# Spacing the four loads of a weight part, and a later limit for the angle tables, in an attention and convolution kernel

## The chip, the cores and the metric

The kernel runs on one core of a Trainium2 chip. The metric is the device time of one execution in microseconds (us). Before the change it is 2664.18 us, the median of three runs (2663.63 to 2665.53).

## What is computed

Four images of 1024 channels and 32 x 32 positions, so 1024 tokens each, go through an attention layer and then a bottleneck of convolutions. All numbers are float32. Shortened:

```python
# layer 0: attention, 16 heads of 64
q, k, v = split(x @ w_qkv.T + b_qkv)
q, k = rmsnorm(rope(q)) * q_norm_w, rmsnorm(rope(k)) * k_norm_w   # rope: rotation by angles
ctx = softmax(q @ k.T * 64 ** -0.5) @ v
x = x + rmsnorm(ctx @ w_proj.T) * norm_out_w
# layer 1: 1x1 (1024 -> 256), 3x3 (256 -> 256), 1x1 (256 -> 1024)
h = relu(bn(conv1(x))); h = relu(bn(conv2(h)))
return relu(x + softplus(residual_scale) * bn(conv3(h)))
```

## The kernel before

**Stages.** Everything runs in one loop over the four images: project q, then k, then v, then attention, then the output projection; the convolutions follow after the last image. The engines work in the order in which the Python program emits their instructions: the order of TensorE, VectorE, ScalarE and GpSimd (Pool) is written out by hand. Each of these takes its own list strictly in turn, so a step that waits holds up all that stands behind it on its engine. SP's queue issues most of the loads; Pool's queue issues the others, and nearly all stores of prepared weights.

**Projections.** Each projection is a product of 1024 x 1024 matrices, made with seven products of 2 x 2 blocks instead of eight (Strassen's way, in Winograd's form). This needs sums of weight blocks. `project` (q and k of the first image) uses one level. There, `operands` (L229) loads four blocks of weights by SP, makes four sums on VectorE (L236 to L239) and stores the results to `wd` in DRAM by Pool (L242). `project2` (all others) uses two levels: seven outer products, `OUTER`, each of seven inner ones, with sums of sums that are kept in `wd2`. The inner weights come by SP: three blocks by `quarter` (L383), from the weights themselves or from `wd`, and four from `wd2` (L472).

**Weight parts.** The sums for `wd2`, and the sums of the v weights for `wd`, are prepared while the first image is projected, and for one part while the second is. Each such part is made by `prepare` (L385, sums L392 to L395, stores L397) or `prepare_blocks` (L401, sums L409 to L412, stores L414). It takes four pieces of 256 KB in a buffer that is free at that time (`rq`, `unused`, `t`, `to`), issues four loads on Pool's queue one after the other, and returns a function `make`, which does four sums on VectorE and four stores on Pool. `unused` lies in the buffer of the first image's k, so the first write to k waits until the stores of `unused` have landed. `prepare_there` (L422 and following) makes sums of what lies in `rq` already.

**Pace.** `product_done` (L257) is called after each product of TensorE and counts the pace: 1 unit a product of four matmuls of 512 columns in `project`, 0.5 units a product in `project2`. `after(n, step)` puts a step on a list; the next call of `product_done` at which the pace has reached the due time emits it. Steps that are due together go in the order of their due times. A step of which the due time is now is not emitted at once, but by the next call. `weight_parts` (L1140) starts part i at `first + i * step` and lets its `make` follow `lag` = 4 units later. The calls that matter:

- first image, q: the four parts of the v weights for `wd`, then the v parts 0, 1 and 6, from pace 8 on, 2.4 apart (L1196); during k, q part 0 (L1209); during v, q parts 6 and 2, 6.5 units apart (L1216)
- second image, q: k part 5 (L1198)

Of the parts that are prepared during attention, by `load_parts`, the loads go by SP's queue.

**Semaphores.** Every DMA of Pool's queue takes one of eight completion semaphores in turn. It waits until the DMA that had the semaphore before, mostly the one eight places ahead in Pool's list, has landed.

**Angle tables.** `rope` (L709) multiplies q or k with tables of sines and cosines, `sinT` and `cosT`. The tables are first multiplied by the inverse norm of each token (L715), so they are spoilt and loaded anew by Pool after the last turn (L729). `pace["tables"]` (L730) is the pace before which the next rope may not start: the pace at the reload plus 3.7.

Of the kernel before, what the change touches and what calls it, by code (L numbers as in the profile page):

```python
# [18 lines left out]
P = 128  # L19
# [15 lines left out]
WQ, WK, WV, WP, W1 = 0, NFB, 2 * NFB, 3 * NFB, 4 * NFB  # L35
# [26 lines left out]
NH = NT // 2  # L62
NG = NT // 2
# [22 lines left out]
def program(ctx, tc, x, wblk, w2, w3, vecs, cos, sin, out, bad):  # L86


    nc = tc.nc
# [26 lines left out]
    def col(name, i=0):  # L116
        return vec[:, COL[name] + i : COL[name] + i + 1]
# [40 lines left out]
    with tc.tile_pool(name=f"st{u}", bufs=2) as st, ExitStack() as s:  # L158
# [14 lines left out]
        def load_tables(queue):  # L173
            for i in range(2):

                queue.dma_start(sinT[i::2, :], sin[1 - i :: 2, :])
            queue.dma_start(cosT, cos)
# [32 lines left out]
        def big_temp(name):  # L210
            return big.tile([P, N], F32, tag="big", name=name)

        def load_x(b, c, rows=range(NT)):
            for i in rows:
                nc.sync.dma_start(xs[b][:, i, half[c]], x[b, i * P : (i + 1) * P, half[c]])
# [33 lines left out]
        pace = {"at": 0, "room": 0.0, "hold": False, "tables": 0.0}  # L249
# [4 lines left out]
        def after(n, step):  # L254
            later.append((pace["at"] + n, step))
# [118 lines left out]
        def quarter(t, base, k, oq, iq, queue=nc.sync):  # L374

            ob, ih = {"A11": (0, 0), "A12": (0, 1), "A22": (1, 1)}.get(OUTER[k], (None, None))
            if ob is None:
                at = base // NT * NG + 2 * oq
                src = wd[at : at + 2, SUMS.index(OUTER[k]), :, iq * QT : (iq + 1) * QT]
            else:  # L380
                at = base + ob * NG + 2 * oq
                src = wblk[at : at + 2][:, :, ih * CH + iq * QT : ih * CH + (iq + 1) * QT]
            queue.dma_start(t.rearrange("p (g f) -> p g f", g=2), src.rearrange("g p f -> p g f"))  # L383

        def prepare(which, base, k, alloc, queue):  # L385

            a11, a12, a21, a22 = a = alloc(f"pre_{which}_{k}")
            for i, t in enumerate(a):
                quarter(t, base, k, i // 2, i % 2, queue)

            def make():
                nc.vector.tensor_tensor(a22, a21, a22, ALU.add)  # L392
                nc.vector.tensor_tensor(a21, a11, a21, ALU.subtract)
                nc.vector.tensor_tensor(a11, a22, a11, ALU.subtract)
                nc.vector.tensor_tensor(a12, a12, a11, ALU.subtract)  # L395
                for m, t in enumerate((a11, a22, a21, a12)):
                    nc.gpsimd.dma_start(wd2[which, k, m], t)  # L397

            return make

        def prepare_blocks(base, g, alloc, queue):  # L401

            a11, a12, a21, a22 = a = alloc(f"blk_{base}_{g}")
            for i, t in enumerate(a):
                ih = i % 2
                queue.dma_start(t, wblk[base + g + NG * (i // 2)][:, ih * NH * P : (ih + 1) * NH * P])

            def make():
                nc.vector.tensor_tensor(a22, a21, a22, ALU.add)  # L409
                nc.vector.tensor_tensor(a21, a11, a21, ALU.subtract)  # L410
                nc.vector.tensor_tensor(a11, a22, a11, ALU.subtract)
                nc.vector.tensor_tensor(a12, a12, a11, ALU.subtract)  # L412
                for o, t in enumerate((a11, a22, a21, a12)):
                    nc.gpsimd.dma_start(wd[base // NT * NG + g, o], t)  # L414

            return make

        def stay(tile, g):

            return lambda name: [tile[:, 2 * o + g // 2, half[g % 2]] for o in (0, 3, 2, 1)]  # L420
# [263 lines left out]
        def inverse_rms(total, eps, scale, name, then):  # L684


            r = temp(f"rms_{name}")[:, :QT]
            row = inv_d[norms_done.pop(0)]

            def root():  # L690
                o = bank("o2" if name in ("q_0", "k_0") else "o1", f"ss_{name}")[:, :QT]
                for q in range(4):
                    nc.tensor.matmul(
                        o[q * QH : (q + 1) * QH, :], ones[:, :QH], total[:, q * QT : (q + 1) * QT],
                        start=True, stop=True,
                    )
                nc.scalar.activation(r, o, AF.Sqrt, bias=eps, scale=scale)
                after(0.5, invert)

            def invert():  # L700
                spend(3 * TT)
                nc.vector.reciprocal(r, r)
                nc.gpsimd.dma_start(row.rearrange("(q t) -> q t", q=4), r[::QH, :])
                nc.gpsimd.dma_start(total, row.partition_broadcast(P))
                after(2.5, then)

            after(4, root)

        def rope(b, dst, total, eps, scale, w, tag, biased=True):  # L709

            def tables():
                for t in (sinT, cosT):
                    nc.vector.tensor_tensor(t, t, total, ALU.mult)  # L715

            def turn(f):
                k, other = dst[:, f, :], big_temp(f"{tag}s_{b}_{f}")
                for i, (t, table) in enumerate(((other, sinT), (k, cosT))):
                    if w is not None:  # L720
                        nc.vector.scalar_tensor_tensor(t, k, w[i][:, f : f + 1], table, ALU.mult, ALU.mult)
                    elif biased:
                        nc.vector.tensor_tensor(t, k, table, ALU.mult)
                    else:
                        nc.vector.scalar_tensor_tensor(t, k, col("bq", f), table, ALU.add, ALU.mult)
                for i in range(2):
                    nc.gpsimd.dma_start(dst[i::2, f, :], other[1 - i :: 2, :], accum_op=ALU.add)
                if f == NT - 1 and (b, tag) != (B - 1, "k"):
                    load_tables(nc.gpsimd)  # L729
                    pace["tables"] = pace["at"] + 3.7  # L730

            def then():
                if pace["at"] < pace["tables"]:
                    after(pace["tables"] - pace["at"], then)
                    return
                waiting.append((4 * TT, tables))
                for f in range(NT):
                    waiting.append((4 * TT, lambda f=f: turn(f)))

            inverse_rms(total, eps, scale, f"{tag}_{b}", then)  # L740
# [391 lines left out]
        def v_room(name):  # L1132
            return kv.tile([P, N // P, C], F32, tag="v", name=name)
# [6 lines left out]
        def weight_parts(parts, first, step, lag, alloc):  # L1140

            for i, part in enumerate(parts):
                after(first + i * step, lambda part=part: after(lag, part(alloc, nc.gpsimd)))

        def pieces_of(tile, cols=NCH):

            at = deque(tile[:, i, h] for i in range(tile.shape[1]) for h in half[:cols])

            def alloc(name):
                at.rotate(-4)  # L1150
                return [at[i] for i in range(-4, 0)]

            return alloc


        parts_of = {
            base: [
                lambda alloc, queue, which=which, base=base, k=k: prepare(which, base, k, alloc, queue)
                for k in range(len(OUTER))
            ]  # L1160
            for which, base in enumerate((WQ, WV, WP, WK))
        }

        def blocks_of(base):
            return [lambda alloc, queue, g=g: prepare_blocks(base, g, alloc, queue) for g in range(NG)]

        vector_and_act = {mybir.EngineType.DVE, mybir.EngineType.Activation}
        regions = ExitStack()
# [12 lines left out]
        room = v_room("rq_0")  # L1181
        for b in range(B):
# [8 lines left out]
            if b == 0:  # L1191
                unused = kp.tile([P, NT, N], F32, tag="k", name="unused")
                parts = [
                    lambda alloc, queue, g=g: prepare_blocks(WV, g, stay(room, g), queue) for g in range(NG)
                ]
                weight_parts(parts + [parts_of[WV][k] for k in (0, 1, 6)], 8, 2.4, 4, pieces_of(unused))  # L1196
            elif b == 1:
                weight_parts([parts_of[WK][5]], 9, 0, 4, pieces_of(room[:, : NT // 2, :]))  # L1198
# [24 lines left out]
            if b == 0:  # L1223
                todo = blocks_of(WP) + [parts_of[WP][k] for k in (0, 1, 6, 2, 3, 4, 5)]
                todo += [parts_of[WQ][k] for k in (1, 3, 4, 5)] + [parts_of[WK][k] for k in (0, 1, 6, 2, 3, 4)]
# [30 lines left out]
            room = v_room(f"to_{b}")  # L1256
# [12 lines left out]
            if b + 1 < B:  # L1269
# [3 lines left out]
                for j in range(NT):  # L1273

                    def load(b=b, i=rows[j]):
                        for c in range(NCH):
                            load_x(b + 1, c, (i,))
# [397 lines left out]
```

## Time and profile before

| view | value |
|---|---|
| median of 3 runs | 2664.18 us |
| profiled execution | 2667.97 us |
| its span, first to last instruction | 2666.2 us |
| mean granted clock of TensorE | 0.997 |
| VectorE waiting for sinT, in 3 places | 14.4 us |
| TensorE idle in the first 30 us (first x) | 5.9 us |
| DMA to landing, loads of rq at 156 us, median | 9.7 us |
| DMA to landing, loads of t at 239 us, median | 8.9 us |
| DMA to landing, stores of w_k_2b at 167 us | 9.2 us |

The first image's q projection fills 6 to 104 us of the span, k 104 to 202, v 202 to 289. The first attention follows. The second image's q projection runs from 612 to 701 us. A DMA's time to landing counts from its issue; most of the DMAs in these stretches move 256 KB. PE in the profile is TensorE, PEld its weight loads, DVE VectorE, ACT ScalarE, POOL GpSimd, and SPq or POOLq is the queue of an issuing engine. A float32 matmul of the program stands as two in the profile, so a product of four shows as x8. Names like `w_k_2b` are tiles: w, projection k, outer row 2, second half of the blocks.

### The profile page before, as it was taken

Reading aid. Unit: us, or ns where it says so; the run is one execution under the profiler, and the core shown is the slowest. Engines: PE = TensorE matmul, PEld = TensorE weight load, DVE = VectorE, ACT = ScalarE, POOL = GpSimd, SP = SyncE. Lnnn points to the kernel's source line nnn. Section 1 sums busy time; section 2 is a strip of 40 time slices with the busy share of each in tenths; the row PEclk is TensorE's granted clock in tenths of the full one; section 3 lists DMA queues with packets and bytes.
Section 4 is the critical chain, followed back from the end, with each engine's and each line's share of the span. In section 5 each row is a group of like instructions: output and inputs, shape, how many; then the busy total and the mean of one; then the engine's idle time right before and its main releaser. Section 6 shows DMA issues by size and latency. Waiting matters only on the chain. (4 is left out here: it accounts for less than half of the span.)

```text
span 2666.2 us, 40828 instructions
## 1 busy us (share of the span) xinstructions
PE 2630.3 (99%) x15434; PEld 1627.9 (61%) x15434; DVE 2144.5 (80%) x2587; ACT 1121.1 (42%) x1568; POOL 480.9 (18%) x588
## 2 busy tenths in 40 slices
PE   9999999999999999999999999999999999999997
PEld 4448533388888333588886333888884335846843
DVE  5677889997798877887888777887988779877987
ACT  2222465533352556333343555233425654312266
POOL 2542243401011221200111222100111222010000
PEclk9999999999999999999999999999999999999999
DMA  7887777766577452456666531665774443583165
GB/s 274 293 256 214 208 245 243 249 204 228 174 193 213 84 101 61 145 156 221 186 190 166 94 74 39 210 202 178 194 212 90 84 105 110 174 280 101 64 237 206
DMA packets 257820, 463.69 MB, mean 174 GB/s; under 512 B 35152, under 2 KB 127872, under 8 KB 257616
## 3 DMA queue, kind: packets, MB, share of 16 engines
q1 hardware_dynamic: 210528, 306.73, 35.7%
q0 software_dynamic: 47088, 154.27, 23.4%
q8 instruction: 125, 2.05, 0.3%
q14 instruction: 79, 0.65, 0.1%
HBM read 327.43 MB, written 97.01 MB: 159 GB/s over the span
## 5 line engine op out<-in xcount | busy, mean ns | idle before, releaser
L794 ACT ACTIVATE p<-sc 128x1024 f32<-128x1024 f32 x512 | 476.3, 1048 | 16.3 <-PE sc L787 16.0
L787 PE MATMUL sc<-q,k 64*64 64x512 f32 x4096 | 453.3, 591 | 0.0
L800 DVE TENSOR_TENSOR den<-den,p 128x1024 f32<-128x1024 f32 x312 | 385.6, 1236 | 33.2 <-DVE den L798 0.5
L807 PE MATMUL cx<-p,to 64*64 64x512 f32 x3072 | 338.2, 589 | 0.0
L787 PEld LDWEIGHTS sc<-q,k 64*64 64x64 f32 x4096 | 149.6, 132 | 293.4 <-ACT p L794 149.1
L807 PEld LDWEIGHTS cx<-p,to 64*64 64x64 f32 x3072 | 117.4, 133 | 212.2 <-issue 211.9
L480 PE MATMUL p_v<-w_v,x 128*128 128x256 f32 x928 | 210.1, 379 | 1.3 <-DVE x L451 1.3
L485 PE MATMUL p_y<-q,w_y 128*128 128x256 f32 x928 | 209.8, 379 | 0.7 <-issue 0.7
L485 PEld LDWEIGHTS p_y<-q,w_y 128*128 128x128 f32 x928 | 176.0, 190 | 27.9 <-issue 4.1
L480 PEld LDWEIGHTS p_v<-w_v,x 128*128 128x128 f32 x928 | 176.1, 190 | 26.6 <-DVE x L451 2.3
L765 POOL TENSOR_SCALAR q<-q,vec 128x512 f32<-128x512 f32 x64 | 124.8, 1976 | 330.2 <-DVE q L764 330.2
L813 ACT COPY q<-cx 128x512 f32<-128x512 f32 x64 | 37.5, 586 | 346.1 <-PE cx L807 346.1
L485 PE MATMUL p_q<-to,w_q 128*128 128x256 f32 x672 | 152.6, 380 | 0.0
L485 PE MATMUL p_k<-to,w_k 128*128 128x256 f32 x672 | 152.2, 379 | 0.0
L485 PEld LDWEIGHTS p_q<-to,w_q 128*128 128x128 f32 x672 | 127.9, 191 | 18.6 <-issue 1.2
L485 PEld LDWEIGHTS p_k<-to,w_k 128*128 128x128 f32 x672 | 127.4, 190 | 18.4 <-issue 1.2
L807 PE MATMUL cx<-p,rq 64*64 64x512 f32 x1024 | 112.7, 589 | 0.0
L1579 PE MATMUL c<-h,w 128*128 128x512 f32 x256 | 110.3, 592 | 0.5 <-ACT h L1482 0.5
L798 DVE TENSOR_TENSOR den<-p 128x1024 f32<-128x1024 f32 x52 | 63.6, 1222 | 53.0 <-ACT p L794 53.0
L485 PE MATMUL p_y<-to,w_y 128*128 128x256 f32 x384 | 90.5, 380 | 4.5 <-DMA w_y<-wdf 4.5
L800 DVE TENSOR_TENSOR den_T<-den_T,p 128x1024 f32<-128x1024 f32 x72 | 88.2, 1225 | 7.5
L480 PE MATMUL p_v<-w_v,t 128*128 128x256 f32 x384 | 90.1, 379 | 1.4 <-DMA w_v<-wdf 1.4
(494 smaller groups left out, 4305.9 us busy)
## 6 DMA issues: line engine op xcount, KB each, us to landing
w_v<-wd2f SPq DMA_DIRECT2D x112, 256.0 KB, 2.9
w_y<-wd2f SPq DMA_DIRECT2D x112, 256.0 KB, 2.7
w_q<-wd2f SPq DMA_DIRECT2D x84, 256.0 KB, 2.8
w_k<-wd2f SPq DMA_DIRECT2D x84, 256.0 KB, 2.7
wd2f<-w_pre POOLq DMA_DIRECT2D x68, 256.0 KB, 4.3
x<-in_x_dram SPq DMA_DIRECT2D x64, 256.0 KB, 5.2
q<-qs POOLq DMA_DIRECT2D x64, 256.0 KB, 5.5
k<-ks POOLq DMA_DIRECT2D x64, 256.0 KB, 4.5
```

What stands on the lines that cost most here:

```text
L480: nc.tensor.matmul(o[:, q].rearrange("p (g f) -> p g f", g=2), r[:, i, q * P : (q + 1) * P], wt[:, :, i, :], skip_group_check=True, **at,)
L485: nc.tensor.matmul(o[:, q], wt[:, q, i, :], r[:, i, :], skip_group_check=True, **at)
L765: nc.gpsimd.tensor_scalar(cx, cx, col("bv", hp), None, ALU.add)
L787: nc.tensor.matmul(sc[keys, j], k_all[d, hp, t * P + keys.start : t * P + keys.stop], q_all[d, hp, at], start=True, stop=bad is not None,)
L794: nc.scalar.activation(p, sc, AF.Exp)
L798: nc.vector.tensor_tensor(d_, probs[0], p, ALU.add)
L800: nc.vector.tensor_tensor(d_, d_, p, ALU.add)
L807: nc.tensor.matmul(o[j * HD : (j + 1) * HD, i], v[keys, t, h0 : h0 + HD], probs[t][keys, j], start=(t == 0), stop=(t == N // P - 1),)
L813: nc.scalar.copy(cx, o[:, 0])
L1579: nc.tensor.matmul(os[i], w3t[k][f // NH][:, f % NH, :], h2[b, k][:, half[c]], start=(k == 0), stop=(k == NPT - 1),)
```

## The change

There are two edits. `prepare` and `prepare_blocks` get a further argument `apart`. Where it is not 0, the load number i of the four is no longer issued on the spot, but handed to `after(apart * i, ...)`. `weight_parts` passes 0.5; its `make` still follows 4 units after the part starts. The parts that are prepared during attention pass nothing, so their loads stay together. The second edit raises the constant of `pace["tables"]` from 3.7 to 4.3. The rest of the diff passes the arguments through.

```diff
+        def one_by_one(loads, apart):
+
+            for i, load in enumerate(loads):
+                if apart:
+                    after(apart * i, load)
+                else:
+                    load()
+
-        def prepare(which, base, k, alloc, queue):
+        def prepare(which, base, k, alloc, queue, apart=0):
 
             a11, a12, a21, a22 = a = alloc(f"pre_{which}_{k}")
-            for i, t in enumerate(a):
-                quarter(t, base, k, i // 2, i % 2, queue)
+            one_by_one(
+                [lambda i=i, t=t: quarter(t, base, k, i // 2, i % 2, queue) for i, t in enumerate(a)], apart
+            )
...
-        def prepare_blocks(base, g, alloc, queue):
+        def prepare_blocks(base, g, alloc, queue, apart=0):
 
             a11, a12, a21, a22 = a = alloc(f"blk_{base}_{g}")
-            for i, t in enumerate(a):
+
+            def load(i):
                 ih = i % 2
-                queue.dma_start(t, wblk[base + g + NG * (i // 2)][:, ih * NH * P : (ih + 1) * NH * P])
+                queue.dma_start(a[i], wblk[base + g + NG * (i // 2)][:, ih * NH * P : (ih + 1) * NH * P])
+
+            one_by_one([lambda i=i: load(i) for i in range(4)], apart)
...
-                    pace["tables"] = pace["at"] + 3.7
+                    pace["tables"] = pace["at"] + 4.3
...
-                after(first + i * step, lambda part=part: after(lag, part(alloc, nc.gpsimd)))
+                after(first + i * step, lambda part=part: after(lag, part(alloc, nc.gpsimd, 0.5)))
```

More of the change, by code (lines that the diff above doesn't have):

```diff
@@ L1157, in program @@
             base: [
-                lambda alloc, queue, which=which, base=base, k=k: prepare(which, base, k, alloc, queue)
+                lambda *a, which=which, base=base, k=k: prepare(which, base, k, *a)
                 for k in range(len(OUTER))
@@ L1164, in blocks_of @@
         def blocks_of(base):
-            return [lambda alloc, queue, g=g: prepare_blocks(base, g, alloc, queue) for g in range(NG)]
+            return [lambda *a, g=g: prepare_blocks(base, g, *a) for g in range(NG)]
         vector_and_act = {mybir.EngineType.DVE, mybir.EngineType.Activation}
@@ L1193, in program @@
                 parts = [
-                    lambda alloc, queue, g=g: prepare_blocks(WV, g, stay(room, g), queue) for g in range(NG)
+                    lambda alloc, *a, g=g: prepare_blocks(WV, g, stay(room, g), *a) for g in range(NG)
                 ]
```

## The prediction

> **What bounds the kernel.** I read the totals of the page first, then what TensorE waited for, then, stretch by stretch, the timelines of Pool, VectorE and TensorE around the loads that move.
>
> ```profile
> span 2666.2 us, 40828 instructions
> ...
> PE 2630.3 (99%) x15434; PEld 1627.9 (61%) x15434; DVE 2144.5 (80%) x2587; ACT 1121.1 (42%) x1568; POOL 480.9 (18%) x588
> ```
>
> TensorE works for 2630.3 of 2666.2 us, so everything that a better schedule can win is 35.9 us, and the change touches only two stretches: the projections of the first image (30 to 290 us) and the q projection of the second (640 to 665 us). The waits of TensorE (its line, who released it: us, times, longest) that lie in these stretches are three:
>
> ```profile
> PE p_q L485 <- DMA w_q<-wdf: 2.1, 1, 2.1
> ...
> PE p_v L480 <- DMA w_v<-wdf: 1.4, 1, 1.4
> ...
> PE pa_k L303 <- DVE w_k_3b L238: 0.2, 1, 0.2
> ```
>
> In the timeline of TensorE (start, duration, in brackets the idle time before) the first two are here:
>
> ```profile
> 250.89 1.97 PE L480 MATMUL p_v<-w_v,t 128*128 128x256 f32 x8 [1.45 <-DMA w_v<-wdf]
> ...
> 658.15 3.38 PE L485 MATMUL p_q<-t,w_q 128*128 128x256 f32 x8 [2.09 <-DMA w_q<-wdf]
> 661.32 2.24 PE L485 MATMUL p_q<-to,w_q 128*128 128x256 f32 x8
> 663.39 1.89 PE L485 MATMUL p_q<-t,w_q 128*128 128x256 f32 x8
> ```
>
> Half a unit of pace, a product of eight such matmuls, is 1.73 us from start to start elsewhere (245.82 to 247.55). From 658.15 it is 3.17 and then 2.07: 1.44 + 0.34 = 1.78 us more are lost after the wait. The table of windows (us, busy time of PE, PEld, DVE, ACT, POOL, then the granted clock) says why:
>
> ```profile
> 658.10:661.00 2.90, 2.85 (x8) 2.29 (x9) 2.83 (x5) 0.00 (x0) 1.47 (x3) 0.59 0.68 262
> 661.00:664.00 3.00, 3.00 (x13) 2.59 (x12) 0.16 (x1) 0.99 (x2) 0.68 (x2) 0.83 0.90 304
> ```
>
> So at most 0.21 + 1.61 (250.89 less 249.28, where the product was due) + 2.09 + 1.78 = 5.7 us can be won.
>
> **Two rules of the Trainium skill.** "TensorE: Matmul & The Clock Gate", section "HAM oscillation", puts the idle gap that costs the clock at some 3.4 us, and the page says that the activity window runs freely, so that the outcome varies. This trace disagrees on the size: a wait of 2.09 us brought 0.59 and 0.83, while one of 2.35 us (2257.5 to 2259.9) left the clock at 1.00. I count 1.78 us as a possible extra on a wait near 2 us, not as certain. "DMA: Bandwidth & Descriptors", section "Queues, rings and completion order", says that each DMA engine takes packets in turn from the queues that have work. The trace fits: where Pool's and SP's transfers meet (242 to 260 us, DMA share 0.86 and up) Pool's loads of t took a median of 8.9 us to land, against 3.0 for the w_v loads of the stage. I therefore expect a moved load to shift the crowding more than to remove it.
>
> **The change, part by part.** *Angle tables.* In the two programs as built, TensorE, VectorE, ScalarE and SP get the same operations in the same order; with the tables' delay alone changed, Pool's list and all waits are the same too. The rope step is never held back by this limit, so 0.6 units more cost 0; nothing has to hide it.
>
> *The loads.* Pool gets the same transfers, 44 of them loads (11 parts of four), but a part's later loads now stand behind other DMAs. A load due at once is issued one product later, so in the first image's q and k projections (one unit, 3.43 us, a product) three loads go a unit later and the fourth two units later; the sums still come 4 units after the part starts. Pool issues in order and uses eight completion semaphores in turn, so a DMA also waits for the one eight places ahead. On VectorE the whole queue waits behind a part's first sum, which needs the fourth load.
>
> 1. q projection, 40 to 115 us: two loads of parts 1 and 3 fall behind the previous part's four stores, those of part 5 behind w_q_3b's. Put in the slot of the store that is there now, the last load of part 1 lands at 52.92 + 8.5 (landing of wdf<-rq) = 61.4, where its sums now start at 58.00: 3.4 us late. After 2.9 us of sums w_q_2b starts at 64.3 instead of 62.62 and is through L238 at 66.4; TensorE wants it at 69.85. Part 3: about 3 us late, w_q_3b at 84 for 87.02. Part 6: 5 us late, before an idle 7.1 us of VectorE at 120.5. ScalarE's first copy of k waits for the store of `unused` to land (108.98) and would go to 114.5, the fourth stays at 118.12 behind TensorE. On the path: 0. Cover: 3.0 to 3.4 us; beyond it each us costs one.
>
> 2. k projection. Here a load moves past four stores:
>
> ```profile
> 156.09 3.58 POOL L383 DMA_DIRECT2D rq<-in_wblk_dram  x4
> ...
> 166.43 0.60 POOL L242 DMA_DIRECT2D wdf<-w_k_2b  x1 [1.40 <-DVE k L321]
> ...
> 168.77 0.54 POOL L242 DMA_DIRECT2D wdf<-w_k_2b  x1 [0.65 <-issue]
> ```
> ```profile
> wdf<-w_k_2b POOLq DMA_DIRECT2D x1, 256.0 KB, 8.7
> ```
>
> The second block is the DMA view of 168.5 to 170: that last store landed after 8.7 us. In the new order the fourth load takes exactly its place in Pool's list, with the same twelve transfers in front; it lands at 168.77 + 8.7 = 177.5. VectorE now goes:
>
> ```profile
> 169.47 0.68 DVE L392 TENSOR_TENSOR rq<-rq 128x512 f32<-128x512 f32 x1
> ...
> 182.09 0.69 DVE L236 TENSOR_TENSOR w_k_3b_s<-w_k_3b,w_k_3b 128x512 f32<-128x512 f32 x1 [5.96 <-DMA wd2f<-rq]
> ...
> 183.55 0.69 DVE L238 TENSOR_TENSOR w_k_3b<-w_k_3b_s,w_k_3b 128x512 f32<-128x512 f32 x1
> ```
>
> L392 would wait until 177.5, 8 us. Behind it on VectorE stand the part's other sums, the last rope turn of q and two sums of squares, 6.5 us of work (169.47 to about 175.95), then 2.15 us from L236 to the end of L238: TensorE would start pa_k at about 186.1 instead of 184.29. The present idle 5.96 us pay for most of it. Cost +1.8. Ends: with a landing two us sooner it is nothing and even the 0.21 goes (the first w_k_2b store gets one load fewer in front, so the last w_k_3b load comes sooner); with 11.0 us, which q<-qs took at 159 to 162, L392 starts at 179.8 and the cost is 4.1, with the slow clock 5.9.
>
> 3. v projection. The loads of t fall behind k<-ks (244.81) and go from 239.0 to about 246. The w_v block that TensorE lacked at 249.28 was issued at about 241, between them, so its wait likely goes: -1.6. What is late next: the block issued at 251.2 for 259.6 now meets them (0 to 1.6 back), and the sums of t, now at 255.22, wait for a landing at 249.5 + 8.9 = 258.4. VectorE has only 1.2 us (269.10) and 2.7 us (286.31) idle until the attention needs the PSUM banks at 289. I take -0.3; ends -1.6 and +1.5.
>
> 4. q projection of image 1: four loads of `to` move past one store of y, from 643.97 to about 646.9. Pool's queue is full either way until 657 (x1df<-y 10.4 us, to 9.2 us to landing), so SP's weight block, needed at 656.06, gains little: I take -0.7, ends -3.9 (wait and clock both gone) and +1.5.
>
> Sum: 0 + 1.8 - 0.3 - 0.7 = +0.8 us. The profiled execution took 2667.97 (span 2666.2, 1.8 around it) and would take 2668.8. The median of the runs is 2664.18, 3.8 lower; the same difference on it gives **2665.0**.
>
> **Rivals.** *A new wait at w_k_3b (slower).* The fourth load lands 11 us after issue, VectorE reaches w_k_3b at 186.3, TensorE waits over 4 us and the clock falls: +5.9, 2670.1. For: the DMA engines are full there, and the sums use up all VectorE's slack. Against: it needs a landing past 179.2 (PE stall over 3.5 plus the clock) as well as no gain elsewhere. It decides from there. *The weights come in time (faster).* Both waits of TensorE for SP's blocks go, and the k stage costs nothing: -5.7, 2658.5. For: both waits stand where Pool's bursts meet SP's loads. Against: point 4, and the slot argument of point 2. *It does nothing that counts.* The waits only change place: 2664.2. For: the share of DMA stays near 1 on both sides of the move.
>
> **How the numbers follow.** No change means here within 0.2%, 5.3 us, which is what a measurement of this kernel can tell. Forecast case (net between -4 and +5): 0.58. Nothing that counts: 0.17. New wait at w_k_3b or at the end of the v stage, past +5.3: 0.22. All weights in time: 0.03 past -5.3. So faster 0.03, same 0.75, slower 0.22. The range leaves out 2 in 10: below, the gains of points 3 and 4 without cost (-3.9), above, the first rival with its clock (+6.3): 2660.3 to 2670.5.
>
> **What would show it.** Right: L392 of rq idle before its start until about 177, L238 of w_k_3b ending near 186, pa_k released by it; p_v at 250 without its wait; the first 150 us of TensorE unchanged. Wrong: a wait of TensorE between 35 and 150 us (point 1 lacked cover), L392 on time (the slot argument fails), waits of p_v or of the first sc that did not exist (point 3), or p_q at 656 without any wait (point 4). A difference of over 6 us outside these stretches would void the account.

## The result, and the profile after

The changed kernel takes 2671.45 us in the median of 8 runs (2667.01 to 2676.41), the kernel before beside it 2663.94 (8 runs): ratio 1.0026, 95% interval 1.0016 to 1.0035. It is slower by about 7 us, outside the forecast range. Set beside the kernel before a second time it gave 1.0019 (1.0012 to 1.0026, 18 runs). The profiled execution of after took 2671.29 us. That of before, 2667.97, is a long one for its kernel, so the two profiles differ by 3.3 us only.

The totals of the page after, then the longest waits of TensorE (engine, tile, line, who released it: us in total, times, longest), without the first load of x:

```profile
span 2669.5 us, 40823 instructions
...
PE 2631.3 (99%) x15434; PEld 1627.9 (61%) x15434; DVE 2143.1 (80%) x2587; ACT 1120.7 (42%) x1568; POOL 481.1 (18%) x588
```
```profile
PE dn L865 <- DVE den L812: 4.5, 5, 1.1
PE pa_k L303 <- DVE w_k_3b L238: 3.9, 1, 3.9
PE p_q L497 <- DMA w_q<-wdf: 2.6, 1, 2.6
```

The wait for w_v (1.4 us before) is gone, the wait for w_q has grown from 2.1 to 2.6, and the wait of `pa_k` for w_k_3b has grown from 0.2 to 3.9. Most lines have moved down by 9 to 12: L401 is the first sum of a part in `prepare`, L392 before. VectorE in the k projection after (start, duration, engine, line, operation, in brackets the idle time before it and what ended it):

```profile
171.55 0.68 DVE L627 TENSOR_TENSOR sqk<-sqk,sq_k 128x512 f32<-128x512 f32 x1
180.21 0.69 DVE L401 TENSOR_TENSOR rq<-rq 128x512 f32<-128x512 f32 x1 [7.98 <-DMA rq<-in_wblk_dram]
...
188.24 0.69 DVE L238 TENSOR_TENSOR w_k_3b<-w_k_3b_s,w_k_3b 128x512 f32<-128x512 f32 x1
```

L401 needs the part's fourth load. Pool's issue of that load, and TensorE behind it:

```profile
172.93 0.72 POOL L383 DMA_DIRECT2D rq<-in_wblk_dram  x1 [0.21 <-issue]
```
```profile
188.98 5.40 PE L303 MATMUL pa_k<-t,w_k_3b 128*128 128x512 f32 x8 [3.95 <-DVE w_k_3b L238]
194.22 3.60 PE L303 MATMUL pc_k<-t,w_k_3b_s 128*128 128x512 f32 x8
```

From `pa_k` to `pc_k` is 5.24 us instead of 3.43, so 1.81 us more go after the wait. The windows of the same execution (stretch, us; busy PE, PEld, DVE, ACT, POOL; granted clock; DMA share; GB/s) show it to be the clock, which stood at 0.50 for 3.4 us of them:

```profile
188.00:191.00 3.00, 2.02 (x3) 0.96 (x4) 2.93 (x6) 0.68 (x2) 2.80 (x6) 0.75 1.07 201
191.00:194.00 3.00, 3.00 (x6) 1.25 (x5) 1.81 (x3) 0.58 (x1) 0.59 (x2) 0.68 0.89 232
194.00:197.00 3.00, 3.00 (x8) 1.33 (x7) 0.00 (x0) 0.59 (x1) 0.00 (x0) 1.00 1.00 393
```

So the place and the kind of the loss are those of point 2 and of the slower rival. From the start of `pa_k<-x,w_k_2b` (173.62 us in before) to that of `pc_k<-x,w_k_3b` (194.70) TensorE takes 21.08 us in before and 26.51 in after, 5.4 us more; from 20 us up to there it takes the same time in both. TensorE's wait is longer than predicted by 1.9 us, the clock comes on top, and VectorE reached L401 at 172.2 instead of 169.5. 1.0 us of this is TensorE's own, which is that much behind before from its first 20 us on. The rest has its origin in the q projection. There the first sums of the v parts wait for their fourth loads, and ScalarE and VectorE come late behind them (timelines of VectorE, then ScalarE, then VectorE):

```profile
81.94 0.69 DVE L421 TENSOR_TENSOR rq<-rq 128x512 f32<-128x512 f32 x1 [7.46 <-DMA rq<-in_wblk_dram]
...
112.43 0.69 DVE L401 TENSOR_TENSOR unused<-unused 128x512 f32<-128x512 f32 x1 [8.99 <-DMA unused<-in_wblk_dram]
```
```profile
121.07 2.05 ACT L311 COPY k<-pa_k 128x512 f32<-128x512 f32 x4 [4.44 <-DMA wd2f<-unused]
```
```profile
136.91 1.23 DVE L727 TENSOR_TENSOR sinT<-sinT,sqq 128x1024 f32<-128x1024 f32 x1 [1.51 <-DMA sqq<-inv_df]
```

Four copies of k stand together at 121.07; the last of them was at 118.12 before. The inverse norms of q follow them, and the product with the table of sines starts at 136.91 instead of 133.91, after a wait that was not there before. TensorE itself does not wait between 35 and 150 us.

### The profile page after: what moved, and what is told of

The parts are those of the page before. It is cut to its first block, busy times and chain, and to the rows that moved or that the text cites. A ratio compares the mean times of both kernels' runs of the same rounds, so it can differ in the third digit from the quotient of the medians.

```text
span 2669.5 us, 40823 instructions
## 1 busy us (share of the span) xinstructions
PE 2631.3 (99%) x15434; PEld 1627.9 (61%) x15434; DVE 2143.1 (80%) x2587; ACT 1120.7 (42%) x1568; POOL 481.1 (18%) x588
## 5 line engine op out<-in xcount | busy, mean ns | idle before, releaser
L739 POOL DMA_DIRECT2D k<-ks x64 | 57.7, 1090 | 180.3 <-ACT p L806 71.1
```

## The experiments

Theory B is mine: q part 0's fourth load makes VectorE late for w_k_3b, and the v parts of the q projection make that wait longer. The first rival, A, puts the whole loss on q part 0's wait; the second, C, on waits that the v parts cause in the q projection. Every run stands beside runs of the kernel before on the same chip, whose median was 2664.18, 2664.68, 2664.16 and 2664.88 us for the four groups of runs below.

### Parts alone

`weight_parts` takes the distance as an argument here, and single calls pass 0.

```diff
-        def weight_parts(parts, first, step, lag, alloc):
+        def weight_parts(parts, first, step, lag, alloc, apart=0.5):
...
-                after(first + i * step, lambda part=part: after(lag, part(alloc, nc.gpsimd, 0.5)))
+                after(first + i * step, lambda part=part: after(lag, part(alloc, nc.gpsimd, apart)))
...
-                weight_parts([parts_of[WQ][0]], 14, 0, 4, pieces_of(room[:, : NT // 2, :]))
+                weight_parts([parts_of[WQ][0]], 14, 0, 4, pieces_of(room[:, : NT // 2, :]), 0)
```

This is e1, which spares q part 0 only. In e2 the 0 stands at every call but that of q part 0, in e3 at every call but that of the v parts; e4 is the kernel before with 4.3 for 3.7. The tables' limit is 3.7 in e2 and e3, and later in e5, e6 and e12 to e14.

> The changed kernel, with the four loads of q part 0 (first image, k projection) issued together again; all other parts stay spaced, tables at 4.3. Theory A (the whole loss is VectorE waiting at q part 0's first sum for its fourth load, so that w_k_3b and TensorE's pa_k come late, with the slow clock behind it): back to the time before or up to 2 us under it, 2662 to 2664; no wait of TensorE for w_k_3b over 1 us. Theory B (two causes add up: the spaced v parts of the q projection bring VectorE some 2.7 us late into the k projection, and q part 0's wait comes on top): also near 2664, with a wait for w_k_3b of 1 to 3 us left. Theory C (the v parts make TensorE wait in the q projection in most runs, which the one profile missed): 2667 to 2670, most of the loss stays.

> The kernel before, with only q part 0 spaced. Theory A: 5 to 8 us slower than before, VectorE waits about 8 us at the first sum of q part 0 and TensorE about 4 us for w_k_3b. Theory B: 1 to 3 us slower, as the prediction had it, VectorE reaches that sum at about 169.5 and TensorE waits about 2 us. Theory C: 1 to 3 us slower.

> The kernel before, with only the seven v parts of the first image's q projection spaced. Theory A: within 1 us of before. Theory B: within 2 us of before, VectorE 2 to 3 us later in the k projection than in the kernel before, TensorE's wait for w_k_3b 0.2 to 2 us. Theory C: 3 to 6 us slower, with a wait of TensorE for w_q_2b or w_q_3b.

> The kernel before, with only the tables' limit at 4.3. All theories: no difference, within 1 us, since the list of every engine is the same as before; it also shows by how much two equal programs differ, and a second profile of this program, in which the waits of TensorE for w_v (1.4 us) and w_q (2.1 us, with 1.8 us of slow clock) may be there or not.

| run | spaced | time, us | ratio (interval) | wait for w_k_3b in the profile, us |
|---|---|---|---|---|
| e1 | all but q part 0 | 2664.9 | 1.0002 (0.9994 to 1.0011) | 0.4 |
| e2 | q part 0 only | 2666.96 | 1.0011 (1.0005 to 1.0018) | 2.7 |
| e3 | the seven v parts only | 2665.42 | 1.0004 (0.9996 to 1.0013) | none |
| e4 | none, tables later | 2663.47 | 0.9999 (0.9990 to 1.0007) | none |

The tables cost nothing that the interval shows. C falls: with the v parts spaced there is no loss that the interval shows (e1, e3). A is too simple for a loss of 7 us: q part 0 alone makes 2.9. But two signs that were named for B did not appear either. In e1 no wait of 1 to 3 us was left, only 0.4. In e3 VectorE was not 2 to 3 us late: it reached L401 14.5 us ahead of TensorE's due time, and 14.6 ahead in before.

### The rest of the parts, and the sums out of the way

e5 spaces q part 0 and the v parts, e6 only the three later parts (q parts 6 and 2, k part 5), e8 is the changed kernel again. e7 leaves all loads of the changed kernel as they are and moves the sums of q part 0 by four units, behind those of w_k_3b:

```diff
-                weight_parts([parts_of[WQ][0]], 14, 0, 4, pieces_of(room[:, : NT // 2, :]))
+                weight_parts([parts_of[WQ][0]], 14, 0, 8, pieces_of(room[:, : NT // 2, :]))
```

> Only the seven v parts of the q projection and q part 0 of the k projection have their loads spaced; the three later parts (k part 5, q parts 6 and 2) load together. Theory B (the two causes work on each other: the v parts bring VectorE late into the k projection, q part 0's load lands later for it, and TensorE's wait for w_k_3b grows from 2.7 to about 4 us, with a slow clock behind it): 2668 to 2672, a wait of 3 to 5 us in the page's k projection. Plain sum of the parts measured alone (2.8 for q part 0, 1.2 for the v parts): 2667 to 2668.5. Third reading (the rest comes from the three later parts, which no run has had alone): about 2666 to 2667, and the next run then shows a loss of its own.

> Only k part 5 and q parts 6 and 2 have their loads spaced. Theory B and the plain sum: 2661 to 2664.5, no change or up to 1.5 us faster, since the wait for w_v (1.2 us in the run with nothing but the tables moved) goes and nothing else does. If the rest of the loss comes from these three: 2665.5 to 2668.

> The changed kernel with the sums of q part 0 four units of pace later, so that VectorE makes w_k_3b first; its loads stay as spaced as they are, on the same queue, and so does everything else. If the cause is VectorE held up in its list by the fourth load (theory B and the prediction's own rival): the wait for w_k_3b falls below 1 us and the time to 2663 to 2667. If it is the transfers themselves (the loads delay others on the queues): the wait stays at 2 to 4 us and the time at 2669 to 2672.

> The changed kernel itself, on the chip of the three others. Theory B: 2669 to 2673, with a wait for w_k_3b of 2.5 to 5 us and the clock down for some 3 us behind it; if the wait was 3.9 us only because that execution began 0.95 us late on TensorE, it is nearer 2.7 here and the time is the same.

| run | time, us | ratio (interval) | wait for w_k_3b, us |
|---|---|---|---|
| e5, q part 0 and v parts | 2669.57 | 1.0019 (1.0011 to 1.0026) | 4.4 |
| e6, later parts only | 2665.31 | 1.0000 (0.9992 to 1.0008) | none |
| e7, sums later | 2664.82 | 1.0004 (0.9996 to 1.0012) | none |
| e8, changed kernel | 2670.02 | 1.0019 (1.0012 to 1.0026) | 2.6 |

e7 settles the mechanism of the wait. Its fourth load is issued at 170.16 and so as late as in e2, but VectorE has w_k_3b ready first. VectorE and TensorE in e7:

```profile
181.41 0.69 DVE L236 TENSOR_TENSOR w_k_3b_s<-w_k_3b,w_k_3b 128x512 f32<-128x512 f32 x1 [8.84 <-DMA sinT<-in_sin_dram]
...
184.80 0.68 DVE L401 TENSOR_TENSOR rq<-rq 128x512 f32<-128x512 f32 x1
```
```profile
183.61 3.70 PE L303 MATMUL pa_k<-t,w_k_3b 128*128 128x512 f32 x8
```

L236 starts 3.4 us before L401 instead of after it, TensorE has no wait, and the clock stays: `pc_k` follows `pa_k` after 3.54 us, as in before. It is VectorE's place in its list behind the load that costs, not the transfer. e6 shows that the later parts neither cost nor win anything that can be told: the wait for w_v is down to 0.4 us in its profile, and `p_v` at 250 us starts 2.0 us sooner than in e4, with which TensorE was 0.6 us ahead already. In the first attention this is given back: TensorE waits for `den` 3.7 us in e6 and 2.4 in e4, and where the output projection begins it is 0.7 us behind e4 (526.01 for 525.31).

### The fourth load's place, and starting earlier

e9 puts only the fourth load of q part 0 back with the third; the list gives the due time of each load, by one more line in `one_by_one`. e10 starts the v parts 1.5 units sooner and leaves their sums where they were; e11 does so with all parts.

```diff
-                after(first + i * step, lambda part=part: after(lag, part(alloc, nc.gpsimd, 0.5)))
+                after(first + i * step, lambda part=part: after(lag, part(alloc, nc.gpsimd, apart)))
...
-                weight_parts([parts_of[WQ][0]], 14, 0, 4, pieces_of(room[:, : NT // 2, :]))
+                weight_parts([parts_of[WQ][0]], 14, 0, 4, pieces_of(room[:, : NT // 2, :]), [0, 0.5, 1, 1])
```
```diff
-                weight_parts(parts + [parts_of[WV][k] for k in (0, 1, 6)], 8, 2.4, 4, pieces_of(unused))
+                weight_parts(parts + [parts_of[WV][k] for k in (0, 1, 6)], 6.5, 2.4, 5.5, pieces_of(unused))
```

> The changed kernel, but the fourth load of q part 0 (k projection) is due with the third, which puts it back ahead of the last rope store and the four stores of w_k_2b in Pool's list; nothing else moves. If the fourth load's place alone makes the wait: no wait for w_k_3b over 0.5 us, 2662.5 to 2666.5. If the spaced v parts of the q projection cost by themselves: 2667 or more, with a wait elsewhere.

> The changed kernel with the seven v parts of the q projection starting 1.5 units of pace earlier and their sums where they were (lag 5.5), so that the fourth loads are due when all four were before. Theory B: VectorE reaches the first sum of q part 0 at about 169.5 us (less or more what TensorE is early or late at its start) instead of 170.2 to 172.6, the wait for w_k_3b is 2.0 to 2.7 and the time about 2667 (2665.5 to 2668.5), as with q part 0 alone. If the v parts do nothing: 2669 to 2671, as the changed kernel.

> All spaced parts start 1.5 units earlier, their sums where they were. If the lateness of the fourth loads is the whole cause and the spacing itself costs nothing: no wait for w_k_3b over 0.5 us, 2661.5 to 2665.5. If the spacing itself costs (transfers spread over other engines' traffic): 2666 or more.

e9: 2666.5 us, 1.0012 (1.0005 to 1.0018), a wait for w_k_3b of 0.3 us. The wait goes with the fourth load's place, as expected, but the time is some 3 us above the kernel before. The profile has TensorE waiting 2.0 us for w_q in the second image with the clock down behind it; whether that holds for the other executions is not known.

e10: 2668.36 us, 1.0015 (1.0009 to 1.0022), a wait of 2.5 us. The profile is as B expects (VectorE is not late, see the table below), the interval cannot tell it from the changed kernel.

e11: 2666.9 us, 1.0008 (1.0000 to 1.0016). The time is that of the second reading, though the interval reaches the kernel before; the first reading, no wait for w_k_3b, is missed. The fourth load is in time and the sums of q part 0 do not wait, but TensorE waits 2.3 us for w_k_3b all the same. VectorE in e11:

```profile
174.26 0.68 DVE L401 TENSOR_TENSOR rq<-rq 128x512 f32<-128x512 f32 x1
...
184.06 0.69 DVE L236 TENSOR_TENSOR w_k_3b_s<-w_k_3b,w_k_3b 128x512 f32<-128x512 f32 x1 [5.54 <-PE pa_k L303]
```

VectorE stood idle for 5.5 us. The line names the product before, but by the packets of SP's queue it was the last load of w_k_3b that VectorE waited for. SP issued it at 176.80, and at 175.80 in before, and from 177.5 to 181 us SP's queue moved 0.11 MB in e11 and 0.30 in before. The issue hangs on Pool again. In all 17 profiles SP issued this load 0.14 us after the first store of w_k_2b had landed, and in e11 Pool issued that store at 167.67 instead of 166.43, 0.55 us after the landing of the part's first load, here as in before; that load took 11.1 us instead of 9.8. This step has no room in either kernel.

### All four corners on one chip

Since single and joint parts had been measured on different chips, e12 (v parts alone), e13 (q part 0 alone), e14 (both) and e15 (the kernel of e7) repeat them on one.

> The seven v parts of the q projection alone spaced, a second time, now on the chip of the three others. If the v parts cost by themselves, as the run with the fourth load put back suggests: 2665.5 to 2667, ratio 1.0005 to 1.001. If they only bring q part 0 late: 2663 to 2665.

> q part 0 alone spaced, a second time, on the same chip. Theory B: a wait for w_k_3b of 2.0 to 2.7 us with the clock down behind it, about 2667 (2666 to 2668.5). If q part 0 makes the whole loss and the rest is chance: 2668.5 to 2670.5, as with both.

> Both spaced, a second time, on the same chip. Theory B: a wait of 2.6 to 4.4 us, 2669 to 2671, more than the sum of the other two over the kernel before by 0.5 to 2 us. Plain sum: equal to it within 0.5 us, with a wait of some 2.6 us.

> The changed kernel with the sums of q part 0 four units later, a second time, on the same chip. If VectorE's place behind the fourth load is the main cause: 2664 to 2666 and no wait for w_k_3b over 0.5 us; what is left over the kernel before is then the v parts' own cost.

| run | time, us | ratio (interval) | wait for w_k_3b, us |
|---|---|---|---|
| e12, v parts | 2664.36 | 1.0001 (0.9993 to 1.0009) | none |
| e13, q part 0 | 2669.07 | 1.0013 (1.0006 to 1.0019) | 2.8 |
| e14, both | 2668.96 | 1.0017 (1.0010 to 1.0023) | 4.6 |
| e15, sums later | 2666.68 | 1.0010 (1.0004 to 1.0017) | 0.3 |

The v parts alone cost nothing that the interval shows, twice. q part 0 alone makes 2.9 and 3.5 us by the ratios, both together 4.5 to 6.9 (four measurements, two of them with the later parts too). The times do not show that the v parts add to q part 0's loss: on this chip the medians of e13 and e14 are the same, and e13 lies in the range of the other reading, in which q part 0 makes the whole loss. The traces show it in part. Every profile with q part 0's fourth load late for VectorE, its times in us:

| profile | fourth load issued | L401 starts | `pa_k` starts | `pa_k` less L401 | VectorE reaches L401, before TensorE is due | wait | lost to the clock |
|---|---|---|---|---|---|---|---|
| e2, q part 0 | 170.73 | 178.07 | 186.84 | 8.77 | 14.5 | 2.66 | 1.81 |
| e13, q part 0 | 170.47 | 177.80 | 186.57 | 8.77 | 14.5 | 2.78 | 1.81 |
| e10, v parts earlier | 171.27 | 178.36 | 187.13 | 8.77 | 14.6 | 2.52 | 1.80 |
| e8, changed | 171.17 | 178.26 | 187.03 | 8.77 | 14.2 | 2.58 | 1.80 |
| after, changed | 172.93 | 180.21 | 188.98 | 8.77 | 12.8 | 3.95 | 1.81 |
| e5, both | 174.29 | 180.72 | 189.50 | 8.78 | 12.5 | 4.42 | 1.67 |
| e14, both | 172.78 | 179.82 | 188.59 | 8.77 | 13.0 | 4.61 | 2.83 |

The timeline of TensorE in e13 and then in e14 shows what the last two columns are read from:

```profile
186.57 5.40 PE L303 MATMUL pa_k<-t,w_k_3b 128*128 128x512 f32 x8 [2.78 <-DVE w_k_3b L238]
191.81 3.60 PE L303 MATMUL pc_k<-t,w_k_3b_s 128*128 128x512 f32 x8
```
```profile
188.59 6.43 PE L303 MATMUL pa_k<-t,w_k_3b 128*128 128x512 f32 x8 [4.61 <-DVE w_k_3b L238]
194.85 3.60 PE L303 MATMUL pc_k<-t,w_k_3b_s 128*128 128x512 f32 x8
```

"Due" is the start of `pa_k` less its wait; before the change VectorE reached this sum 14.6 us ahead of it. "Lost to the clock" is the start of `pc_k` less that of `pa_k`, less 3.43. Once the load has landed the rest is rigid, 8.77 us in all seven. TensorE's way past this place, the 21.08 us of before, is 20.6 to 21.3 us in the nine profiles without a wait of over 0.4 us here, and 25.1 to 28.2 in these seven.

The size of the wait hangs on when the fourth load is issued, and that on the semaphores of Pool's queue. In the trace the fourth store of w_k_2b has the semaphore of the part's first load, eight places ahead, and the fourth load has that of the second. In all seven profiles, and in e7 and e15, the store is issued 0.51 us after the first load has landed, and the fourth load 0.28 us after the second has, or as soon as the store is out (after: 171.67 and 172.18, then 172.65 and 172.93). Where the wait is short, the first load was issued at 158.6 to 159.5 us; in after, e5 and e14 at 160.5 to 161.9, behind rope stores that wait for VectorE's turns.

In those three VectorE came 1.5 to 2.0 us nearer to TensorE's due time than with q part 0 alone, and the wait is 3.95 to 4.61 us; in the fourth profile with both, e8, it was hardly late, and the wait is as short as with q part 0 alone. The product with the table of sines shows the same: against TensorE it is 1.6 to 2.1 us late in those three, which are the three in which ScalarE's copies of k came latest. In the other seven profiles with the v parts spaced at their old start it is late by 0.3 us at most, and in the seven without by nothing. So the v parts lengthen the wait in some executions and not in others.

e15 keeps 1 to 4.5 us over the kernel before with a wait for w_k_3b of 0.3 us only, as e9 did, while e7, the same kernel, showed none that counts; the intervals of e7 and e15 overlap. e15's own profiled execution (2662.81 us) is 3.9 below its median, so its trace does not show where the rest is. This stays open.

A hint is in the second image: in the eight profiles in which k part 5 is spaced at its old start, TensorE's wait for w_q is 1.7 us in the mean (0.4 to 2.6) and its way from 620 to 700 us, the clock included, 78.2; in the eight that load it together, 1.1 (0.4 to 2.1) and 77.4. The single profiles scatter by about 1 us, and no run had k part 5 alone, so this is argued and not shown.

## Why the prediction was wrong, point by point

- *Angle tables, 0.* Right (e4, 0.9999).
- *Point 1, "On the path: 0. Cover: 3.0 to 3.4 us".* Right for TensorE in the q projection, though with less to spare than computed: L421 started at 62.16 for 61.4, then at 81.94 for some 78.5, and w_q_3b was made at 86.87 where TensorE wanted it at 87.97. Wrong for what stands behind it. The last sums of `unused` start at 112.43, 12 us late and not 5, so that ScalarE copied k at 121 and the fourth copy did not "stay at 118.12". The point ended at ScalarE and did not follow the inverse norms of q to the rope and into point 2.
- *Point 2, +1.8.* This is the term that failed, in two steps: the slot argument, by which the fourth load would be issued at 168.77 in the place of the store, and the clock that was left out. The chain behind the landing was right: 8.6 us predicted from there to `pa_k`, 8.77 measured. (VectorE's work ends at 176.13 in the timeline of before, and not at "about 175.95".) The place in the list was right too, but not when its turn comes: store and load wait there for the landings of the part's own first and second loads, and those had moved a unit later themselves. The prediction names the semaphores and does not apply them. With q part 0 alone the fourth load was issued at 170.5 and 170.7 and landed after 7.3 us instead of 8.7, at 177.8 and 178.0 for 177.5; that two errors nearly cancel there is luck. With both it was issued at 171.2 to 174.3 and landed at 178.2 to 180.7. The slow clock, which the forecast called possible near 2 us and left out of the central sum, came in every profile with the wait, for 1.7 to 2.8 us. Wait and clock together are 4.5 and 4.6 us with q part 0 alone and 4.4 to 7.4 with both, in place of 1.8. These are single executions, in e2 and e13 2.1 and 2.7 us above the medians, and the times show 2.9 to 3.5 us for q part 0 alone. Where the wait is longer than with q part 0 alone, the added part goes with point 1's lateness.
- *Point 3, -0.3, and point 4, -0.7.* The wait for w_v did go, as said, but the later parts together gave 1.0000 (e6), so what was won was given back. In the means of the same two groups of eight profiles TensorE's way is 1.1 us shorter from 235 to 255 us, 0.9 longer from 300 to 610, where it waits for `den`, and 0.8 longer from 620 to 700, where point 4 expected a gain; the scatter makes the last two uncertain. In after the wait for w_q was 2.6 us and not shorter.
- *The rivals.* "A new wait at w_k_3b (slower)" is what happened, at 2670.1 predicted and 2668.96 to 2671.45 measured for both parts together. Its trigger was wrong: it asked for a landing of 11 us after issue, past 179.2. The load landed after 6.4 to 7.3 us; it was the issue that came late, and a landing at 177.8 was enough for a wait with slow clock.
- *The rule on the clock.* The Trainium skill, "TensorE: Matmul & The Clock Gate", section "HAM oscillation", gives an idle gap of some 3.4 us as the limit, which would leave all waits of 2.5 to 2.8 us free. The four of them at this place cost 1.8 us each. The measurement decides: here the clock belonged in the central sum.

## What to carry to other kernels

When a load moves in an in-order list, follow the engine that waits for it, and what is queued behind the waiting instruction there, to the next step that has no slack. Ask also which earlier transfer has to land before the moved one may be issued: here it was one of the same part, which had moved as well. Emit the sums of something that is not urgent behind those of something that is (e7), and TensorE no longer waits for the late load. A point that ends with "late, but covered" has to hand its lateness on to the next point of the sum, since two covers that each suffice are used by the same engine. And add the clock to any predicted wait of TensorE that is near the size of one that already cost it.

## What was not expected of the hardware

At w_k_3b a wait of 2.3 to 4.6 us was followed by slow clock in eight of eight profiles (the seven and e11). Each time the granted clock was 0.50 for 3.41 us, in e14 for 6.83, and the fall began between 1.3 us before the restart (e14) and 1.4 us after it (e10). Elsewhere the length of the wait alone does not tell: one of 2.64 us at 665.76 in after had no slow clock, and one of 2.00 us at 657.11 in e7 lost 1.79 us on the next two products. In the 17 profiles together, from 30 us on and from 1.2 us upward, none of the 27 waits of TensorE up to 1.82 us had a fall behind it, 9 of the 18 from 1.86 to 2.64 us had one, and all five of 2.66 us and more.

The first 32 matmuls of the kernel, before any of the moved loads, took from 15.4 us (e3) to 17.0 us (after), so that TensorE was up to 1.6 us apart where the programs are still the same.
